# Delta-rule planes stored in pairs, tokens ordered by blocks of four steps, and the whole instruction order written down as a table

## The chip, the cores and the metric

The kernel runs on one core of a Trainium2 chip. Its time is the device time of one execution in microseconds; for the kernel before it is the median of three runs. Lower is better. Profiles are of single executions with the hardware profiler on.

## The reference

The input `x` is 8 sequences of 512 steps with 128 features. Four layers follow one another, each added to its input:

1. a gated linear recurrence over the steps (per channel, `z = a*z + b*u`, with coefficients from the normalised input, and with two weight matrices divided by their largest singular value where that exceeds 1);
2. one linear map, chosen from eight by an argmax over constants;
3. attention by the delta rule with 16 heads of size 8;
4. a mixture of experts: 8 experts 128 to 512 to 128 with a gelu, the best two per token, weighted by their probabilities.

The third layer matters most here. Per head and sequence it keeps an 8 x 8 state:

```
retrieval = einsum('bhij,bhj->bhi', S, k_t)
S = S + einsum('bhi,bhj->bhij', beta_t * (v_t - retrieval), k_t)
o_t = einsum('bhij,bhj->bhi', S, q_t)
```

All data are float32.

## The kernel before

**Tiling.** The 512 steps are cut into 32 tiles of 16 steps (`QT`); a tile has 8 sequences x 16 steps = 128 tokens (`QN`). Eight groups of four tiles (`SIZES`) pass through the layers in turn. The first layer (`scanned`, L814, `ssm_out`, L894), the second (`linear`, L900) and the preparation of the third (`delta_in`, L919) work on a group of 512 tokens at once. Their arrays have features on the partitions and tokens along the free axis, or the reverse after PE transposes. Before all that, two serial chains of 25 matrix squarings (`spectral`, L1445) find the two largest singular values; the second layer's input (`gain`) needs them.

**The recurrence.** `delta_rule` (L1013) works through the tiles in blocks of four steps (`BL`), so 4 blocks a tile and 128 in all. The 128 partitions are 16 heads x 8 rows `i` of the state; the columns of the state are 8 "planes" `j`. `delta_in` writes the normalised queries and keys to DRAM (`scratch`), and two transfers per tile read them back into `kq`, spread so that each partition of a head has all 8 features: 16 planes of 128 tokens. A block is six DVE instructions, each needing the one before it:

- `so = kq * state`: the state at the block's start times keys and queries, 16 planes x 32 tokens = 512 elements;
- `w = sum over planes of so`: the eight key planes and one plane of values (`vals`), nine addends for 32 tokens;
- `prod = tmat * w` and `u4 = sum(prod)`: a prepared 4 x 4 triangular matrix per head resolves the four steps of the block;
- `st = k * u4` and a sum that adds the four steps to the state.

`so` is one array of 26 planes. A plane is 128 neighbouring words, so the nine addends of one token lie 512 bytes apart. Even and odd tiles use different planes for queries and for `vals`, and the same ones for keys. `vals` comes into its plane by a transfer from SP's queue for each tile. After a tile's four blocks, ACT copies `u_16` (the four `u4`) from PSUM to `upd`, POOL multiplies `upd` with the prepared products of queries and keys (`qkp`), from tile 8 on (`PRESUM`) POOL also adds the two halves of the eight query planes of `so`, from tile 28 on also adds `qkp` to them, and PE sums the remaining planes with the output weights `wo` in PSUM. DVE adds the residual (`x3 = po + base`), for each tile, as a step of its own (L1086, the last lines of `delta_rule`).

**Routing and experts.** `route` (L1089) chooses the experts of a group. `experts` (L1190) runs for one group, then three times for two groups, then for the last group (`GROUPS`). It gives every token two places in a table sorted by expert, POOL scatters the rows there with indirect transfers (`places`, L1260), 128-row blocks are loaded (`xb`), their expert's first weights are loaded by a register (`w1b`, five buffers), PE makes the hidden layer (`ph`), ACT the gelu (`hid`), PE the second layer (L1322), ACT copies it (`yb`) and SP stores it (`results`). POOL gathers each token's two rows with indirect transfers (`back`), and POOL or, for the last groups, DVE adds them with their weights into `fin` or `acc`, which goes to `out` by one transfer per tile. There are 99 blocks: 15, 23, 23, 23 and 15.

**What sets the order.** [...] The kernel records all operations first (`Recorder`, L291, `Plan.add`, L112) with what they read and write. `Plan.best` (L189) then places them by `place` (L204): a list scheduler that picks per engine by a rank, with costs from `_cost` (L340) and with due times from a table of one number per stage (`DUE`); `backward` (L144) makes ranks from a first placing. `BURST` and `WINDOW` (L359) can hold indirect transfers apart; here they are 1 and 0, no limit. The four shared PSUM banks (`Bank`) are assigned there too. `emit` (L280) issues everything in that order. Nearly every instruction therefore carries line 316, that of the recorder, and is told apart by its tiles.

**Loads and stores.** A tile of `u` is read by one transfer of 64 KB (`rows_of`, L512, in `load_x`, L516); the token on partition p is sequence p // 16, step p % 16. Each group is read twice, once early for its layer-norm statistics (into a `w1b` buffer) and once for the work. All these are on SP's queue.

Of the kernel before, what the change touches and what calls it, by code (L numbers as in the profile page):

```python
# [9 lines left out]
F32 = mybir.dt.float32  # L10
# [3 lines left out]
ALU = mybir.AluOpType  # L14
AX = mybir.AxisListType

P = 128
# [52 lines left out]
class Plan:  # L70
# [117 lines left out]

    def best(self):  # L189

        stages = sorted({op.key[0] for op in self.ops})
# [148 lines left out]
def _cost(engine, name, n, kw):  # L340
# [7 lines left out]
    if engine == "scalar":  # L348
        columns = sum(isinstance(kw.get(k), bass.AP) for k in ("bias", "scale"))
        return 0.18 + 0.00085 * n + (0.0, 0.0001 * n, 0.13)[columns]  # L350
# [8 lines left out]
BURST, WINDOW = 1, 0.0  # L359
# [5 lines left out]
DUE = (  # L365
    -236, -276.1, -245.3, -238.7, -88.4, -98.3, -52.3, -79.1, -157.5, -15.6, -71, 7.4, -42.8, -28.1, 23.8, 17.7,
    3.3, 15.3, -94.2, -33.2, 126.6, -87.6, -36.7, 39.7, -104.5, -21.9, 9.6, 53.8, 21.8, 117.2, 17.2, 34, 105.7,
    174.3, -88.9, 90.1, 19.1, 146.3, 93.6, 29.9, 38.9, 28.9, 34.5, 209.9, 195.2, 91.1, 102.7, 46.1, 1.8, 95.7,
    -4.3, 89.8, 13.7, 74.3, 96.5, 3.1, 90.5, 77.5, 38.7, 101.6, 143.2, 40.1, -66.1, 12.2, -5.1, 212.4, 20.7, 101.5,
    73.5, 98.5, 116.8, 100.9, 78.2, 3, 102.1, 38.3, 290.5, 128.1, 214.1, 180.9, 131.2, 128, 118.3, 113.8, 15.2,  # L370
    14.5, 225.5, 100.6, 218.2, 210.7, 114.8, 91.1, 105.7, 127.4, 209.4, 212.9, 96.9, 226.6, 177.7, 246.3, 250.5,
    289.6, 287.3, 210.3, 152.1, 215.7, 247.3, 234.5, 176.6, 304.3, 235, 219.2, 187.8, 232.7, 315.6, 194, 205.6,
    295.7, 240.7, 326.7, 206.2, 233.2, 183.6, 211, 284.8, 261.9, 245.8, 311.8, 194.9, 361.5, 272, 302.9, 248,
    136.1, 193.7, 231.9, 225.4, 248.8, 243.7, 247.5, 303.1, 282.2, 193.1, 316, 265, 251.8, 321, 335.7, 373.6,
    307.1, 296.4, 323.7, 318.1, 304.2, 306.2, 317.4, 323.4, 286.7, 304.5, 314.1, 305.1, 311.8, 307, 281.3, 273.9,
    304.9, 267.2, 326.6, 310.3, 341.2, 222.4, 327.2, 320, 342, 274.2, 348.8, 375.1, 433.6, 289.9, 271.2, 406.7,
    316.1, 313, 282.7, 390.3, 246.2, 305.4, 298.8, 320.5, 298.3, 282.6, 219, 458.7, 284.2, 368.8, 326, 305.3,
# [13 lines left out]
def seq_kernel(  # L391
# [120 lines left out]
    def rows_of(dram_, tile):  # L512

        return dram_[:, tile * QT : (tile + 1) * QT, :]
# [1087 lines left out]
```

## Time and profile before

| | us |
|---|---|
| median of 3 runs (lowest, highest) | 699.95 (699.14, 700.88) |
| the profiled execution, its own time | 700.99 |
| its span, first to last instruction | 699.3 |
| busy: PE / DVE / ACT / POOL | 511.3 / 500.4 / 455.1 / 546.4 |
| first block of the recurrence starts | 95.5 |
| last block of the recurrence ends | 591.8 |
| last matmul ends | 681.7 |
| DMA engines' share in use on queue q1 | 51.0% |

"Busy" is the sum over an engine's instructions. A group of instructions reads: line, engine, operation, tile written <- tiles read, shape out <- shape in, count, then busy us and mean ns of one, then the idle time of the engine just before them and what ended it. "issue" is time in which the profile shows no wait. The rows of the page that the prediction shows are not shown again here.

The chain that ended last begins at 647 and is PE's work on the last experts, then POOL's gathers, then DVE's last adds:

```profile
679.89 0.48 ACT yb L316
...
692.33 0.30 issue
692.64 2.87 DMA back<-results,small_dest
...
695.60 0.35 DVE acc L316
```

### The profile page before, as it was taken

What the parts mean: (1) busy time and instruction counts of PE and PEld (TensorE: products, weight loads), DVE (VectorE), ACT (ScalarE), POOL (GpSimd) and SP (SyncE); (2) the same over time, 40 slices, a digit from 0 to 9 for tenths busy, and PEclk for the clock granted to TensorE, in tenths of its full rate; (3) what the DMA queues carried; (4) which work ended last, traced back from release to release, by engine and by line L of the source; (5) the groups of instructions that cost most, each with busy time, mean ns of one, the idle gap of its engine ahead of it and who ended that gap; (6) DMA issues with size and microseconds to landing.
All of it is one profiled execution on the core that took longest, in us unless ns stands there. A gap on an engine that the chain in (4) does not pass through costs nothing. (4 is left out here: it accounts for less than half of the span.)

```text
span 699.3 us, 10984 instructions
## 1 busy us (share of the span) xinstructions
PE 511.3 (73%) x2948; PEld 402.0 (57%) x2948; DVE 500.4 (72%) x1276; ACT 455.1 (65%) x1052; POOL 546.4 (78%) x681
## 2 busy tenths in 40 slices
PE   6883656755783767898569979947799968996990
PEld 5662225433551435677427746836568858986980
DVE  4771199999985999998969999975999987400013
ACT  4987765668763578798495789834675734863660
POOL 7588755896579879898869999977589788777644
PEclk9885686997776689998867997977999989999995
DMA  3492243532264357563557665544787876776762
GB/s 105 132 303 77 62 112 96 129 77 64 65 164 133 87 139 172 154 174 83 139 163 187 176 162 150 148 117 122 209 207 206 244 211 171 207 238 195 211 194 70
DMA packets 97714, 105.92 MB, mean 151 GB/s; under 512 B 9099, under 2 KB 72534, under 8 KB 97654
## 3 DMA queue, kind: packets, MB, share of 16 engines
q1 hardware_dynamic: 92992, 96.66, 51.0%
q0 software_dynamic: 4160, 8.53, 4.3%
q8 instruction: 25, 0.41, 0.3%
q14 instruction: 35, 0.29, 0.1%
q10 hardware_dynamic: 502, 0.03, 0.0%
HBM read 81.26 MB, written 23.94 MB: 150 GB/s over the span
## 5 line engine op out<-in xcount | busy, mean ns | idle before, releaser
L316 ACT ACTIVATE hid<-ph,w1b 128x128 f32<-128x128 f32 x396 | 113.5, 375 | 51.7 <-issue 17.3
L316 PE MATMUL ph<-xbT,w1b 128*128 128x128 f32 x792 | 113.6, 286 | 7.8 <-ACT hid L316 3.6
L316 PEld LDWEIGHTS ph<-xbT,w1b 128*128 128x128 f32 x792 | 103.3, 199 | 21.0 <-ACT hid L316 8.9
L316 DVE TENSOR_TENSOR so<-kq,st 128x512 f32<-128x512 f32 x128 | 87.6, 684 | 7.0 <-DVE st L316 1.1
L1322 PE MATMUL po<-w_sb,hid 128*128 x616 | 86.6, 281 | 6.6 <-ACT hid L316 5.0
L316 DVE TENSOR_REDUCE st<-so 128x32 f32<-128x288 f32 x128 | 84.3, 658 | 3.2
L1322 PEld LDWEIGHTS po<-w_sb,hid 128*128 128x128 f32 x616 | 78.2, 195 | 11.8 <-ACT hid L316 7.3
L316 POOL DMA_INDIRECT back<-results,small_dest x64 | 62.3, 973 | 26.5 <-issue 16.0
L316 PE MATMUL po<-wo,so 128*128 128x128 f32 x304 | 56.5, 344 | 34.1 <-POOL so L316 21.6
L316 PEld LDWEIGHTS po<-wo,so 128*128 128x128 f32 x304 | 51.4, 251 | 49.3 <-POOL so L316 24.8
L1260 POOL DMA_INDIRECT places<-xne,small_dest x64 | 63.9, 998 | 19.0 <-issue 13.3
L316 DVE TENSOR_REDUCE st<-st 128x64 f32<-128x320 f32 x128 | 63.8, 498 | 9.4 <-ACT upd L316 5.2
L316 PE MATMUL in<-b,head_ones 128*128 128x512 f32 x80 | 47.8, 684 | 17.1 <-ACT vals L316 3.4
L285 ACT ACT_TABLE_LOAD x42 | 53.9, 1283 | 6.1 <-DMA hid<-in_L_ffn_b_dram 5.4
L316 DVE TENSOR_TENSOR st<-kq,st 128x256 f32<-128x256 f32 x128 | 54.8, 428 | 4.3
L316 PE MATMUL in<-b,wqkvb 128*128 128x512 f32 x64 | 41.2, 739 | 17.9 <-ACT b L316 6.9
L316 POOL TENSOR_TENSOR qkp<-qkp,upd 128x512 f32<-128x512 f32 x32 | 37.8, 1181 | 12.7 <-ACT upd L316 12.6
L316 PEld LDWEIGHTS po<-wo,qkp 128*128 128x128 f32 x224 | 33.5, 222 | 22.7 <-POOL qkp L316 18.0
L316 PE MATMUL po<-wo,qkp 128*128 128x128 f32 x224 | 36.5, 310 | 13.2 <-POOL qkp L316 13.2
L316 PE MATMUL in<-f,wT 128*128 128x512 f32 x64 | 37.7, 676 | 11.4 <-DVE drive L316 6.0
L316 DVE TENSOR_REDUCE st<-prod 128x32 f32<-128x128 f32 x128 | 37.7, 294 | 9.8 <-ACT upd L316 3.8
L316 DVE TENSOR_TENSOR prod<-tmat,st 128x128 f32<-128x128 f32 x128 | 36.6, 286 | 10.7 <-POOL tmat L316 6.5
(285 smaller groups left out, 1207.0 us busy)
## 6 DMA issues: line engine op xcount, KB each, us to landing
kq<-scratch SPq DMA_DIRECT2D x64, 512.0 KB
w1b<-w1b_dram SPq DMA_DIRECT2D x99, 258.0 KB
xb<-places SPq DMA_DIRECT2D x21, 256.0 KB
results<-yb SPq DMA_DIRECT2D x21, 256.0 KB
places<-yb SPq DMA_DIRECT2D x2, 1472.0 KB
x<-in_L_attn_u_dram SPq DMA_DIRECT2D x32, 64.0 KB
w1b_dram<-in_L_ffn_w_dram SPq DMA_DIRECT2D x1, 2048.0 KB
scratch<-qn SPq DMA_DIRECT2D x8, 256.0 KB
```

What stands on the lines that cost most here:

```text
L285: self.hw.scalar.preload_act_table_set(switch)
L316: return method(*(on(x) for x in args), **{k: on(x) for k, x in kw.items()})
L1260: rows_out = hw.gpsimd.indirect_dma_start(out=table[0 : nblk * P, :], out_offset=bass.IndirectOffsetOnAxis(ap=at, axis=0), in_=src, in_off ...
L1322: return hw.tensor.matmul(out_.on(nc.banks), lhsT=src, rhs=w2_f[:, bass.ds(at + c * P, P)], start=(c == 0), stop=(c == NHB - 1),)
```

## The change

- **Planes in pairs.** `so` becomes two sets (even and odd tiles) of 9 pairs of planes. Two planes of a pair are interleaved word by word: 8 query planes, 8 key planes, and a pair of `vals` and zeros. `so = kq * state` writes every second word; the sum reads five pairs, ten addends, over two axes. PE's weight loads of query planes read every second word.
- **`vals`** comes into its plane by an ACT copy, where a transfer did it.
- **Tokens by blocks.** The token on partition p of a tile is now block p // 32, sequence (p % 32) // 4, step p % 4; a block's 32 tokens are neighbours in `kq`, `so` and `tmat`. `u` is reordered accordingly: for the first group by 16 small loads, alternately from SP and ACT; for the others by one transfer from DRAM to DRAM (`u_rows`) that both later loads read. `out` goes the other way round: one store of a group to `out_rows` and one transfer from there, and for the last group 16 small stores.
- **Buffers.** `xb` 3 to 2, `w1b` 5 to 4, and a temporary of `delta_in` shares another's buffer.
- **The order.** `ORDER` lists the numbers of all recorded operations; `ordered` follows it and gives out the PSUM banks, the one that has been free longest. `DUE` is empty, and the list scheduler doesn't run. `BURST`, `WINDOW` and one cost of `_cost`, which only it reads, change too.

```diff
+    def ordered(self):
+        order, loaded, freed = [], None, list(range(-len(self.banks), 0))
+        for at, number in enumerate(ORDER):
+            op = self.ops[number]
+            for b in op.begins:
+                b.index = min(b.choice, key=freed.__getitem__)
+                freed[b.index] = len(ORDER)
+            for b in op.ends:
+                b.users -= 1
+                if b.users == 0:
+                    freed[b.index] = at
+            switch = op.table if op.table and op.table != loaded else None
+            loaded = switch or loaded
+            order.append((op, switch))
+        return order
...
     def best(self):
+        if len(ORDER) == len(self.ops):
+            return self.ordered()
...
-BURST, WINDOW = 1, 0.0
+BURST, WINDOW = 4, 6.0
...
+    def in_blocks(dram_, g):
+        steps = dram_[:, FROM[g] * QT : FROM[g + 1] * QT, :]
+        return steps.rearrange("b (k t) d -> k b (t d)", t=BL)
+    def blocks_in(rows):
+        return rows.rearrange("q (k b t) d -> (q k) b (t d)", b=B, t=BL)
...
     def load_x(g):
         x = ptile([P, SIZES[g], D], "x", 2)
+        if g:
+            nc.sync.dma_start(x, u_rows[g].rearrange("q p d -> p q d"))
+            return x
         for i in range(SIZES[g]):
-            nc.sync.dma_start(x[:, i], rows_of(u, FROM[g] + i))
+            for k in range(QB):
+                by = nc.sync if k % 2 == 0 else nc.scalar
+                by.dma_start(x[k * B * BL : (k + 1) * B * BL, i], block_rows(u, FROM[g] + i, k))
...
-    so = ctile([P, 26 * QN], "so")
+    so = ctile([P, 2, 2 * DH + 2, QN], "so")
+    nc.gpsimd.memset(so[:, :, 2 * DH :], 0.0)
...
-            nc.sync.dma_start(so[:, v0 * QN : (v0 + 1) * QN], vals[:, cols_q])
-            for x, src in ((xk, scratch[1, q]), (xq, scratch[0, q])):
+            now = so[:, (FROM[g] + q) % 2].rearrange("p x c -> p (x c)")
+            def pairs(x):
+                return now[:, 2 * x * QN : 2 * (x + 1) * QN].rearrange("p (c e) -> p c e", e=2)
+            nc.scalar.copy(pairs(DH)[:, :, 0], vals[:, cols_q])
+            for x, src in ((1, scratch[1, q]), (0, scratch[0, q])):
...
-            so_r = so[:, w0 * QN : (w0 + 9) * QN].rearrange("p (r b t) -> p b t r", b=B, t=QT)
+            so_v = now[:, 0 : 2 * DH * QN].rearrange("p (x c e) -> p x e c", c=QN, e=2)
+            so_r = now[:, DH * QN :].rearrange("p (x c e) -> p c x e", c=QN, e=2)
...
-                nc.vector.tensor_mul(so_v[:, :, :, ts], kq_v[:, :, :, ts], state)
-                nc.vector.tensor_reduce(w, so_r[:, :, ts, :], AX.X, ALU.add)
+                nc.vector.tensor_mul(so_v[:, :, :, ts], kq_v[:, :, ts], state)
+                nc.vector.tensor_reduce(w.rearrange("p b t -> p (b t)"), so_r[:, ts], AX.XY, ALU.add)
...
-            outs = [so[:, (q0 + d) * QN : (q0 + d + 1) * QN] for d in range(DH)]
+            outs = [pairs(d // 2)[:, :, d % 2] for d in range(DH)]
...
+    def rows_out(g, acc):
+        nc.sync.dma_start(out_rows[g].rearrange("q p d -> p q d"), acc)
+        nc.sync.dma_start(in_blocks(out, g), blocks_in(out_rows[g]), group="rows")
...
-                xb = ptile([P, 4, D], "xb", 3)[:, 0:m]
+                xb = ptile([P, 4, D], "xb", 2)[:, 0:m]
...
-            w1b = ptile([P, FW], "w1b", 5)
+            w1b = ptile([P, FW], "w1b", 4)
```

## The prediction

> **What bounds the kernel now.** I read the 40 slices and the costliest groups of the page first, then the groups by form, then the windows by stage, and last the timelines around the long waits.
>
> ```profile
> DVE  4771199999985999998969999975999987400013
> POOL 7588755896579879898869999977589788777644
> ...
> L316 DVE TENSOR_TENSOR so<-kq,st 128x512 f32<-128x512 f32 x128 | 87.6, 684 | 7.0 <-DVE st L316 1.1
> L316 DVE TENSOR_REDUCE st<-so 128x32 f32<-128x288 f32 x128 | 84.3, 658 | 3.2
> L316 DVE TENSOR_REDUCE st<-st 128x64 f32<-128x320 f32 x128 | 63.8, 498 | 9.4 <-ACT upd L316 5.2
> ```
>
> DVE fills the slices from about 90 to 590 us. There it runs a serial chain of 128 blocks (32 tiles of four); one block is six instructions, 684 + 658 + 286 + 294 + 428 + 498 = 2848 ns, and 128 of them 364.5 us. The first starts at 95.5, the last ends at 591.8. So I cut the span into start 95.5, recurrence 496.3, tail 107.5 (699.3 in all); the profiled run's own time, 700.99, has 1.7 more around the span and lies 1.0 above the median of 699.95.
>
> ```profile
> 108.10:589.30 481.20, 358.32 (x2027) 277.26 (x2025) 422.42 (x1011) 321.21 (x704) 399.27 (x495) 0.85 0.56 149
> ```
>
> Columns are window, PE, PEld, DVE, ACT, POOL. From the first to the last product of `qkp`, DVE is busy 422 of 481 us, POOL 399, and POOL's waits add 15.8 us of "issue" after indirect transfers: 415. POOL is second, at 86%. DVE's waits over 0.25 us in the recurrence sum to 29.9 us; four of them, 6.1, 5.2, 3.8 and 8.1, make 23.2. The longest:
>
> ```profile
> 473.70 0.29 DVE L316 TENSOR_TENSOR prod<-tmat,st 128x128 f32<-128x128 f32 x1
> 482.10 0.29 DVE L316 TENSOR_TENSOR x<-po,base 128x128 f32<-128x128 f32 x1 [8.11 <-PE po L316]
> ```
> ```profile
> 473.28 0.97 POOL L1260 DMA_INDIRECT places<-xne,small_dest  x1 [0.30 <-issue]
> 474.56 1.01 POOL L316 DMA_INDIRECT back<-results,small_dest  x1 [0.30 <-issue]
> 475.59 1.27 POOL L316 TENSOR_TENSOR so<-so 128x512 f32<-128x512 f32 x1
> 477.03 1.00 POOL L1260 DMA_INDIRECT places<-xne,small_dest  x1 [0.17 <-issue]
> 478.05 1.20 POOL L316 TENSOR_TENSOR qkp<-qkp,upd 128x512 f32<-128x512 f32 x1
> ```
>
> An add on DVE stands in line for a PE sum, whose `so` and `qkp` planes POOL makes late, behind a train of indirect transfers of 1.27 us each. The other three long waits have such trains beside them too.
>
> [...] From 128 to 320 elements DVE reductions go 294 to 498 ns, 1.06 ns an element on 158 fixed; `st<-so`, whose nine addends lie 512 bytes apart, should take 464 and takes 658. The steps of `tmat` show both cases:
>
> ```profile
> L316 DVE TENSOR_TENSOR b<-b,b 128x128 f32<-128x128 f32 x4 | 1.9, 527 | 0.0
> L316 DVE TENSOR_TENSOR b<-b,beta 128x384 f32<-128x384 f32 x1 | 1.1, 1105 | 10.8 <-ACT b L316 10.8
> L316 DVE TENSOR_TENSOR b<-b,beta 128x256 f32<-128x256 f32 x1 | 0.4, 404 | 0.0
> ```
>
> [...] the product `so<-kq,st` (one PSUM input) stays within 656 to 690 ns over 128 runs, so a busier POOL won't stretch the chain. [...]
>
> **The change, part by part.**
>
> *Reduction by pairs.* `st<-so` now reads five pairs, 320 elements (a zero plane is added)[...]. Value: the row of `st<-st`, also 320, 498 ns. 128 x (658 - 498) = 20.5 us, all in the chain. Bounds: the old excess of 194 ns over 288 elements is 0.67 ns each; if 320 still pay it, 158 + 340 + 215 = 713, +7.0 us in all; a cheaper case than 498 is excluded by the 1.06 ns slope.
>
> *The product writes every second word.* Same 512 elements. [...] Bounds: the excess of 0.67 ns on each would be 343 ns a block, 128 x 0.343 = +44 us; below nothing is excluded, since 684 is already the plain slope (rows of 512 from PE sums also take 680). The other four instructions keep size and count.
>
> *`vals` by an ACT copy.* 32 SP issues of 0.53 us go; 32 copies at the row of `upd` (128x128, 264 ns) come, 8.4 us on ACT, busy 321 of 481. In the built order a tile's copy stands two tiles ahead of its first reduction, before the `upd` copy of two tiles earlier: a cover of about 11 us. It waits for the reduction that last read that plane; queued behind it are the `upd` copy and an activation run. Without cover, 0.3 to 0.5 us a tile, up to +16. I take 0. PE loads `so` planes at a stride of two words: 0, bounded by 128 x 0.67 ns on 160 loads per pass, some 27 us of an engine with 123 us free.
>
> *Tokens by blocks, `u` and `out` in two steps.* 60 loads of 64 KB become 16 small ones and 7 reorderings in DRAM with 14 loads; 28 stores become 7 of 256 KB plus 7 reorderings. That adds some 7.3 MB (7 x 256 KB written and read once more, for `u` and `out`) to 105.9, at a DMA share of 56%: covered, since loads run a group ahead; uncovered each costs some 3 us of landing. But eight of the first loads stand ahead on ACT's queue: its ten issues took from 0.81 to 5.38, 0.46 each, so +3.7; two small steps move behind (-0.7), and ACT idled 1.1 before its first squaring. 1.9 us late, and the squarings are serial: +1.9 (0 to 3).
>
> *Buffers.* `w1b` 5 to 4, `xb` 3 to 2. Four blocks are 4 x 8 matmuls x 0.22 = 7 us of PE, a late `w1b` took 3.9 to land: 0; without that cover 1 to 2 us per late block.
>
> *The table.* It moves work on all queues. The PE order is nearly the same at the end: after the last `so` sum 152 first-layer, 152 second-layer matmuls and 38 transposes, before 144, 152 and 34: +2.7 us at 0.22 a matmul (two of the half passes, of which the chain of waits has 16 in 1.79 us). On POOL the last scatter stands 5.1 us of work later (48.0 after the last `qkp` product where it was 42.9, summed from rows), PE waited 3.6 + 2.1 us there already: +4. The `fin` adds no longer stand behind the last `acc` sum, which held the last gathers to 683.7: -0.7; the last stores on two queues +0.2. Tail +3.5. In the recurrence dependent DVE steps stand further apart, and adds of late sums sit up to twelve blocks after their tile. But indirect transfers are no sparser: at most 11 in any 15 us of POOL work, 10 before, and POOL's work runs up to 20 us behind DVE's (8 before). I let a third of the 23.2 us go: -7.7; bounds -20 and +10.
>
> Sum: 700.99 + 1.9 - 20.5 - 7.7 + 3.5 = 678.2 for a profiled run, 677 as a median.
>
> **Rivals.**
> - *POOL takes over.* DVE's own work falls to some 447 us; POOL's 415 of 481 becomes 415 of 453, 92%, with its trains. What is late next is `qkp` and `so`, then the `upd` copy. Waits grow by 3 in place of falling by 7.7: about 688. For it: the lag of 20 us. Against: adds placed late.
> - *The table cures the waits.* 20 us of them go: 665. For it: all four have one cause; against: the trains remain.
> - *Strided write pays.* At the bound, 677 + 44 = 721: slower. It decides from an excess of 0.19 us a product, (700 - 677)/128, a product of 0.87 us. [...]
> - *Pairs don't help* (the 1105 ns row is the hint): reduction 713 ns, 677 + 20.5 + 7.0 = 704.
>
> **How the numbers follow.** Forecast 0.44, POOL 0.25, cured 0.20, strided write 0.07, pairs 0.04. Below 0.3% (2.1 us) a measurement of this kernel can't tell a change from none. Slower: 0.11; of the POOL case 0.03 reaches 698 to 702; faster 0.86. The range 660 to 694 takes in the first three cases, less their outer ends (0.08), and leaves out 0.11.
>
> **What would show it.** `st<-so` at about 500 ns, 128x320 (wrong at 600 or more); `so<-kq` within 680 to 700; recurrence of 460 to 476 us from the first to the last block; first block at 97; tail of 110 to 112; DVE's long waits near 22 us, named for PE, ACT `upd` or POOL. If POOL takes over, they name POOL `qkp` and `so` and exceed 30. Wrong altogether if the product exceeds 0.87 us, or if waits of the reduction for ACT `so` appear in every tile.

## The result, and the profile after

| | before | after |
|---|---|---|
| median of 15 runs each (lowest, highest) | 701.0 (699.14, 703.48) | 694.65 (690.79, 699.55) |
| the profiled execution, its own time | 700.99 | 694.65 |
| its span | 699.3 | 693.0 |
| start, to the first block | 95.5 | 101.0 |
| recurrence, first to last block | 496.3 | 467.7 |
| tail, from the last block on | 107.5 | 124.3 |

The ratio is 0.991, with a 95% interval of 0.989 to 0.993: faster by 0.9%, where 677 and thus 3.3% had been forecast. The time lies 0.65 us beyond the slow end of the range. The recurrence became shorter by 28.6 us, start and tail longer by 5.5 and 16.8. The recorder's line is 335 in the kernel after, and 340 or 345 in some kernels below.

First the page of the kernel after, the rows that answer to those of before: the slices of DVE and POOL, and the three largest groups of the chain.

```profile
DVE  4565169999997899995899999878999970300111
POOL 5566776699899979998869999987898886786634
...
L335 DVE TENSOR_TENSOR so<-kq,st 128x512 f32<-128x512 f32 x128 | 87.9, 687 | 13.1 <-POOL small_mine L335 7.8
...
L335 DVE TENSOR_REDUCE st<-so 128x32 f32<-128x320 f32 x128 | 63.1, 493 | 4.8
L335 DVE TENSOR_REDUCE st<-st 128x64 f32<-128x320 f32 x128 | 63.6, 497 | 4.0
```

The sum over pairs takes 493 ns where it took 658, and the product, which now writes every second word, 687 where it took 684. The new thing in these rows is the idle time: 7.8 us ahead of one product, named for POOL.

The windows of the recurrence, before and after (columns: window, its length, then busy time of PE, PEld, DVE, ACT, POOL, the granted clock, DMA share, GB/s):

```profile
95.50:591.80 496.30, 367.05 (x2062) 283.58 (x2061) 435.48 (x1039) 330.36 (x723) 406.00 (x503) 0.85 0.55 146
```
```profile
101.00:568.70 467.70, 354.83 (x1988) 270.29 (x1986) 416.77 (x1039) 338.53 (x743) 403.58 (x504) 0.88 0.56 147
```

DVE has 1039 instructions in both. It is busy 18.7 us less and idle 9.9 us less (60.8 before, 50.9 after): together the 28.6. PE has 74 instructions fewer here. They come back in the tail, where the groups of PE by form after the last block show them, before and after:

```profile
L316 PE MATMUL ph<-xbT,w1b 128*128 128x128 f32 x293 | 41.0, 284 | 4.3 <-ACT xbT L316 2.1 <-DMA w1b<-w1b_dram 1.5 <-ACT hid L316 0.6
L1322 PE MATMUL po<-w_sb,hid 128*128 x184 | 24.6, 277 | 0.4 <-ACT hid L316 0.4
```
```profile
L335 PE MATMUL ph<-xbT,w1b 128*128 128x128 f32 x328 | 52.5, 291 | 8.9 <-DMA w1b<-w1b_dram 7.0 <-ACT xbT L335 0.9 <-ACT yb L335 0.7
L1595 PE MATMUL po<-w_sb,hid 128*128 x242 | 37.9, 281 | 0.1
```

A record is a half pass of a matmul: the 99 blocks have 396 first-layer matmuls, and the whole trace 792 records of them. With the second layer's sums under the name `in` (120 and 88), which are not shown, the experts' half passes are 597 before and 658 after: 61 of the 73 that PE has more there. The windows from the last block to the last matmul, before and after, give PE's time:

```profile
591.80:681.70 89.90, 80.37 (x658) 77.10 (x656) 12.12 (x47) 56.40 (x179) 62.04 (x66) 0.96 0.71 207
```
```profile
568.70:673.70 105.00, 92.42 (x731) 87.70 (x731) 12.67 (x56) 62.08 (x196) 69.06 (x71) 0.95 0.73 209
```

Of the 15.1 us more, PE is busy 12.0 and idle 3.1 (12.6 in place of 9.5). Its 73 instructions more, at 80.37 / 658 = 0.122 us each, are 8.9 of the 12.0.

### The profile page after: what moved, and what is told of

It reads as the page before. It is cut to its first block, busy times and chain, and to the rows that moved or that the text cites. A ratio compares the mean times of both kernels' runs of the same rounds, so it can differ in the third digit from the quotient of the medians.

```text
span 693.0 us, 10892 instructions
## 1 busy us (share of the span) xinstructions
PE 514.9 (74%) x2948; PEld 399.2 (58%) x2948; DVE 483.1 (70%) x1276; ACT 465.4 (67%) x1087; POOL 546.3 (79%) x682
## 5 line engine op out<-in xcount | busy, mean ns | idle before, releaser
L335 PE MATMUL ph<-xbT,w1b 128*128 128x128 f32 x792 | 127.9, 292 | 13.3 <-DMA w1b<-w1b_dram 8.0
L335 PEld LDWEIGHTS ph<-xbT,w1b 128*128 128x128 f32 x792 | 112.1, 205 | 25.0 <-issue 11.2
L1595 PE MATMUL po<-w_sb,hid 128*128 x704 | 114.4, 288 | 5.2 <-DVE small_place L335 1.4
L1595 PEld LDWEIGHTS po<-w_sb,hid 128*128 128x128 f32 x704 | 99.1, 201 | 15.7 <-issue 7.5
L335 DVE TENSOR_TENSOR so<-kq,st 128x512 f32<-128x512 f32 x128 | 87.9, 687 | 13.1 <-POOL small_mine L335 7.8
L335 POOL DMA_INDIRECT back<-results,small_dest x64 | 61.9, 968 | 32.9 <-DMA results<-yb 16.2
L335 PEld LDWEIGHTS po<-wo,so 128*128 128x128 f32 x264 | 45.5, 239 | 36.4 <-issue 17.7
L335 DVE TENSOR_REDUCE st<-so 128x32 f32<-128x320 f32 x128 | 63.1, 493 | 4.8
L335 PE MATMUL po<-wo,so 128*128 128x128 f32 x264 | 51.8, 333 | 19.1 <-DVE x L335 7.9
L335 PE MATMUL in<-f,wT 128*128 128x512 f32 x64 | 41.8, 750 | 10.8 <-DVE x L335 4.4
L335 DVE SCALAR_TENSOR_TENSOR fin<-back,small_weight,fin 128x128 f32<-128x128 f32 x16 | 5.1, 349 | 57.4 <-DMA back<-results,small_dest 50.1
L335 POOL TENSOR_TENSOR so<-so 128x512 f32<-128x512 f32 x24 | 30.7, 1280 | 12.1 <-DVE so L335 10.7
```

The lines of the kernel that those rows point to most:

```text
L335: return method(*(on(x) for x in args), **{k: on(x) for k, x in kw.items()})
L1595: return hw.tensor.matmul(out_.on(nc.banks), lhsT=src, rhs=w2_f[:, bass.ds(at + c * P, P)], start=(c == 0), stop=(c == NHB - 1),)
```

## What was tried

Three questions: what the 7.8 us wait is and what it costs; what made the start 5.5 us later; why PE has more left at the end. The table has the stages of a profiled execution of most kernels; those with other buffers, other places for loads or half the columns are told in the last part. On two of the chips (one of them marked *) every kernel, the one before included, took some 30 us longer (the one before 733.89 and 730.69, on the others 699.96 to 701.88), with stops common to several engines in the tail, of up to 17 us: there only the ratio and the stages up to the last block are compared with other chips.

| kernel | first block | recurrence | last matmul after it | median | ratio to before, 95% |
|---|---|---|---|---|---|
| before | 95.5 | 496.3 | 89.9 | 701.0 | |
| after | 101.0 | 467.7 | 105.0 | 694.65 | 0.991 (0.989 to 0.993) |
| after, again | 101.4 | 467.3 | 103.6 | 693.71 | 0.990 (0.985 to 0.994) |
| POOL held to the table* | 99.7 | 460.4 | 126.2 | 709.36 | 0.967 (0.962 to 0.972) |
| first loads all on SP* | 105.2 | 466.9 | 129.0 | 722.9 | 0.985 (0.980 to 0.991) |
| last copy first* | 99.8 | 472.9 | 127.1 | 720.84 | 0.981 (0.976 to 0.986) |
| first group in two transfers | 98.3 | 468.4 | 105.2 | 691.78 | 0.986 (0.983 to 0.990) |
| POOL held, and two transfers | 98.5 | 461.5 | 100.2 | 680.92 | 0.971 (0.967 to 0.975) |
| the same, again | 100.2 | 459.5 | 102.0 | 681.81 | 0.973 (0.969 to 0.976) |
| nine planes apart | 100.4 | 478.3 | 102.5 | 704.53 | 1.007 (1.005 to 1.009) |
| ten planes apart (one run) | 101.3 | 483.7 | 102.9 | 708.93 | |
| new layout, old scheduler | 105.6 | 523.9 | 101.0 | 749.99 | 1.073 (1.070 to 1.076) |

### The wait for POOL

The timelines around it, of POOL, ACT, PE and DVE, of the kernel after (start, duration, instruction, idle time before it):

```profile
311.94 1.10 POOL L1533 DMA_INDIRECT places<-xne,small_dest  x1 [0.17 <-DVE st L335]
...
322.18 0.96 POOL L1533 DMA_INDIRECT places<-xne,small_dest  x1 [0.31 <-issue]
323.16 2.48 POOL L335 TENSOR_TENSOR both<-f,f 128x512 f32<-128x512 f32 x2
```
```profile
325.68 1.06 ACT L335 ACTIVATE both<-both 128x1024 f32<-128x1024 f32 x1 [8.58 <-POOL both L335]
326.64 1.25 ACT L335 ACTIVATE f<-in,dbias 128x512 f32<-128x512 f32 x2
```
```profile
327.94 0.80 PE L335 MATMUL in<-wo,so 128*128 128x128 f32 x2 [9.08 <-ACT f L335]
...
328.96 1.49 PE L335 MATMUL in<-wo,so 128*128 128x128 f32 x6
```
```profile
322.24 0.50 DVE L335 TENSOR_REDUCE st<-st 128x64 f32<-128x320 f32 x1
330.54 0.69 DVE L335 TENSOR_TENSOR so<-kq,st 128x512 f32<-128x512 f32 x1 [7.80 <-POOL small_mine L335]
```

Nine scatters follow one another, 1.27 us each with the 0.30 of "issue". POOL's `both`, of a later group's first layer, stands behind them; ACT waits 8.58 us for it and then, with `f`, empties a PSUM bank (`in`); PE waits 9.08 us for that and then sums a tile's `so` planes, until 330.45. Counted through, DVE's next product is the first of tile 15 (of 0 to 31), which writes the set of planes that this sum, of tile 13, reads. It starts at 330.54, after 7.80 us. The profile names POOL's `small_mine`, which ended at the same moment; in the kernel with the planes apart, below, it puts the like wait (6.67 us) down to PE `in`. That the product waits for this sum is read from the four timelines; the profile does not say it. The table has at most four scatters in a row. In the trace of the program as built there are trains of nine and seven: the scatters of a group are declared independent of one another, and then nothing holds a scatter that stands directly behind another one to its place, so that it is built ahead of POOL's other work. On POOL, then, the order is not the table's. The experiment makes it so: a scatter waits, in issue order only, for what stands ahead of its run of scatters.

```diff
                 made = op.emit()
                 if op.engine == "gpsimd":
-                    self.tc.keep_in_program_order(made)
+                    for name in behind if op.group is None else behind[:1]:
+                        self.tc.add_manual_dep(made.ins, name, issue, reason="the table's order")
+                    behind = [made.ins.name] if op.group is None else behind + [made.ins.name]
```

> POOL's queue as built does not follow the table: a row scatter that the table puts directly behind another row scatter is free to move ahead, so nine of them stand in a row at 312 us and eight at 555, where the table has at most four. This kernel holds POOL to the table and changes nothing else. My theory: DVE's wait of 7.80 us at 330 goes or falls below 3, PE's wait of 5.66 us for the sum planes `so` of the last tile but one goes; recurrence 461 to 463 in place of 467.7, tail 118 to 120 in place of 124.3; 682 to 685 in place of 694.65. Rival 1, the tail is plain PE work (61 more expert matmuls than before behind the last block) and POOL only fills gaps: recurrence as above, tail 123 to 125, about 689. Rival 2, POOL is short of time and the waits only move: 694, long DVE waits still above 20 us.

The wait is gone and the recurrence is 460.4. PE's wait of 5.66 us for `so` at the end is now two, of 1.26 and 1.08. What it gains in the whole is measured below, on a chip without the common stops.

### The start

ACT's timeline from the first instruction to the first squaring, before and after:

```profile
0.81 0.55 ACTq L316 DMA_DIRECT2D hid<-in_L_attn_bp_dram  x1
...
8.02 0.40 ACT L316 ACTIVATE xne<-acc,sp 128x128 f32<-128x128 f32 x1 [1.12 <-DVE sp L316]
```
```profile
0.81 6.34 ACTq L335 DMA_DIRECT2D x<-in_L_attn_u_dram  x8
7.19 0.64 ACTq L335 DMA_DIRECT2D hid<-in_L_attn_bp_dram  x1
...
12.57 0.40 ACT L335 ACTIVATE xne<-acc,sp 128x128 f32<-128x128 f32 x1
```

The eight issues of `u` took 6.34 us, 0.79 each, and all that ACT did followed 6.4 us later. If only ACT's queue were the trouble, they could go to SP:

```diff
-                by = nc.sync if k % 2 == 0 else nc.scalar
+                by = nc.sync
```

> All sixteen first loads of `u` are issued by SP; ACT's queue begins with its ten small loads as before the change. My theory: ACT's first squaring step starts at 8.0 to 8.5 in place of 12.57, the first block of the recurrence at 96 to 97 in place of 101.0, and all of it is passed to the end: 690. Rival 1, SP's own queue takes the place: the first rows and weights land 4 us later, the first block stays at 100 to 101, 694. Rival 2, the start is 5 us earlier and the tail that much longer, since PE's backlog of experts is what ends: 693 to 695.

The first block came at 105.2, some 4 us later than with both queues: the rival holds. SP's timeline of this kernel says why:

```profile
1.28 0.86 SPq L335 DMA_DIRECT2D x<-in_L_attn_u_dram  x1
2.18 0.39 SPq L335 DMA_DIRECT2D acc<-in_L_attn_W_in_dram  x1
2.61 4.22 SPq L335 DMA_DIRECT2D x<-in_L_attn_u_dram  x6
6.88 0.44 SPq L335 DMA_DIRECT2D hid<-in_L_attn_Wp_dram  x1
```

The weights `Wp` go out at 6.88, behind seven small loads. Sixteen small issues cost 0.7 to 0.9 us each on either queue, so the number has to fall: for the first group too, one reordering in DRAM and one load.

```diff
-        if g:
-            nc.sync.dma_start(x, u_rows[g].rearrange("q p d -> p q d"))
-            return x
...
+        if g == 0:
+            nc.sync.dma_start(blocks_in(u_rows[g]), in_blocks(u, g))
+        nc.sync.dma_start(x, u_rows[g].rearrange("q p d -> p q d"))
...
+ORDER = (1, 0, 2, 4, 3) + tuple(n - 14 for n in ORDER if n > 18)
```

> The first group of `u` comes by one reordering transfer in DRAM and one load, as the other groups do, in place of sixteen small loads; ACT's queue begins with its ten small loads. My theory after the run with all sixteen on SP: what costs is the issue of sixteen small transfers, 0.79 us each on either queue (6.34 us for eight on ACT), and who issues them only decides who waits. Here two issues take their place: first squaring step of ACT at 8.0 to 9.0 in place of 12.57, first block at 96 to 98 in place of 101.0, 3 to 5 us off the total. Rival: the two hops land so late (7 to 9 us) that DVE, whose statistics of `u` stand ahead of the squarings' scale, starts the squarings at 11 to 12 all the same: first block at 100 to 101, total unchanged.

The first block came at 98.3, the time fell by 1.9, where 3 to 5 had been expected, against the kernel after on the same chip (its own repetition follows).

> The changed kernel once more, unaltered, as the measure for the kernels beside it. The chip of the four runs before was slower in the tail of every kernel, the kernel before among them (733.9 in place of 701.0), with stops of PE, ACT and SP together of up to 17 us that the first profiles don't have. If that is the chip, this kernel gives 0.991 of the kernel before on a chip like the first, and about 0.98 on one like the second; its recurrence is 467 to 469 us on either.

It gave 693.71, the first result again. So 3 us of start gave 2 in the end, within what two medians differ by.

### Both edits together

> POOL held to the table, and the first group by two transfers. Without stops in the tail: first block at 96 to 98, recurrence 460 to 461 (it was 460.4 with POOL held to the table, 467.7 without), tail 118 to 121 where PE's wait of 5.66 us for `so` is gone; 677 to 681 on a chip like the first, 0.97 of the kernel before. If the tail is PE's backlog alone, every us that the recurrence ends earlier is a us more of tail, and the total stays within 3 us of the changed kernel's.

680.92, as expected, and 681.81 in a repetition below. PE's waits for the last two `so` sums did not go altogether: they are 3.15 and 1.98 us here, the second in the tail. POOL's timeline at the same place, and DVE's group of products over the page:

```profile
311.60 1.10 POOL L1537 DMA_INDIRECT places<-xne,small_dest  x1 [0.16 <-DVE st L340]
...
314.27 0.96 POOL L1537 DMA_INDIRECT places<-xne,small_dest  x1 [0.30 <-issue]
315.25 2.49 POOL L340 TENSOR_TENSOR both<-f,f 128x512 f32<-128x512 f32 x2
317.70 1.18 POOL L340 TENSOR_TENSOR qkp<-qkp,upd 128x512 f32<-128x512 f32 x1
```
```profile
L340 DVE TENSOR_TENSOR so<-kq,st 128x512 f32<-128x512 f32 x128 | 87.9, 687 | 4.8 <-DVE st L340 0.8
```

Three scatters, then `both` and `qkp`; PE's sum of `so` starts at 320.04 and DVE's product after it waits only 0.19 us. Over the page, idle time ahead of the product falls from 13.1 to 4.8. DVE's waits over 0.25 us in the recurrence sum to 11.8 us (29.9 before, 23.2 after). This version beats both kernels: of the 13 us that it gains over the kernel after, the one with two transfers alone has 2, so holding POOL to the table is worth about 11. The kernel before has trains too, of seven, six, six and five scatters; no run holds its POOL to its own order, so what the same edit would be worth there is not known.

### What the pairs are worth

The kernel after with nine planes that lie side by side, as before, and all else kept:

```diff
-            def pairs(x):
-                return now[:, 2 * x * QN : 2 * (x + 1) * QN].rearrange("p (c e) -> p c e", e=2)
+            def plane(x):
+                return now[:, x * QN : (x + 1) * QN]
...
-            so_r = now[:, DH * QN :].rearrange("p (x c e) -> p c x e", c=QN, e=2)
+            so_r = now[:, DH * QN : (DH + 9) * QN].rearrange("p (x c) -> p c x", c=QN)
```

> The changed kernel with the pairs undone and all else kept: every plane of `so` is 128 neighbouring words again, the product writes them without stride and the reduction reads nine addends 512 bytes apart. Theory of the pairs: `st<-so` takes 650 to 665 ns for 288 elements in place of 493 for 320, the product stays at 684 to 690, the recurrence is 20 to 21 us longer, 488; total 710 to 715, or less if the tail then has less left over. Rival, the chain has slack in it: recurrence below 478.

The reduction takes 662 ns (row below), as before the change, and the chain 21 us more (groups of the recurrence: 364.4, 343.2). The recurrence takes 478.3, only 10.6 more, just beyond the rival's bound of 478 and far from the 488 of the theory; the median is 704.53, where 710 to 715 had been expected. Its window shows where the rest is:

```profile
L335 DVE TENSOR_REDUCE st<-so 128x32 f32<-128x288 f32 x128 | 84.7, 662 | 4.8
```
```profile
100.40:578.80 478.40, 357.01 (x1988) 270.68 (x1987) 432.94 (x1039) 339.68 (x743) 404.15 (x506) 0.88 0.54 144
```

Against the kernel after, DVE is busy 16.2 us more, not 21, since its small instructions beside the chain took less (92.8 in place of 97.8, summed from the groups); and it is idle 45.5 in place of 50.9. Its waits over 0.25 us sum to 17.5 in place of 23.2. So part of what the shorter chain saves is waited for.

Ten planes apart, the element count of the pairs without their layout:

```diff
-            so_r = now[:, DH * QN : (DH + 9) * QN].rearrange("p (x c) -> p c x", c=QN)
+            so_r = now[:, DH * QN : (DH + 10) * QN].rearrange("p (x c) -> p c x", c=QN)
```

> As the kernel with the planes apart, but the reduction reads ten of them (the plane of zeros too), the 320 elements that the pairs read. If every element of an unpaired reduction pays the excess of 0.67 ns, `st<-so` takes 710 to 720 ns; if the excess is a fixed one of about 195 ns for the instruction, 690 to 697.

```profile
L335 DVE TENSOR_REDUCE st<-so 128x32 f32<-128x320 f32 x128 | 91.8, 717 | 4.8
```

717 ns for 320 elements apart, 493 for 320 in pairs: the layout alone is worth 224 ns, and the penalty goes by the element, as the prediction's bound of 713 had it.

### What the table is worth

The new layout, without the table, and with the due times and limits of before:

```diff
-BURST, WINDOW = 4, 6.0
+BURST, WINDOW = 1, 0.0
...
+ORDER = ()
```

> The changed kernel without its table: the list scheduler runs with the due times, costs and limits of the kernel before, on the new layout, with four buffers. If the tail's extra length is the table's choice: first block at 98 to 102, recurrence 474 to 480 (496.3 less the reduction's 20.5, waits of 25 to 33 us), tail 108 to 113, 683 to 692. If a faster chain leaves PE that much more of the experts' work in any order: the same recurrence, tail 118 to 126, 692 to 703.

749.99, which neither theory had: recurrence 523.9, first block 105.6, DVE's long waits 63.7 us, the largest 11.65 (ACT `upd`) and 9.89 (PE `po`). Due times that were found for one layout do not fit another, so this run does not price the table by itself. It shows that the layout with the old due times is 7% slower than before. Its tail is long as well: 118.5 us, with 634 of the experts' half passes after the last block.

### The end of the table, and the tail

The first suspect was a late copy of the last `upd` on ACT (576.93), with the last add behind it:

```diff
+ORDER = moved(ORDER, 4566, 4564)
```

> The last tile's copy of `u_16` to `upd` on ACT, which started at 576.93 behind an experts' copy although its data were there at 567.7, is put ahead of that copy; nothing else moves. Theory of ACT's queue: the last residual add comes 8 us earlier, tail 115 to 117, 686. Theory of PE's queue (mine): the last sum on PE stands behind some 60 expert matmuls that PE worked without a gap from 571.1 to 580.4 and can't start before them; the copy was late for nobody: tail 123.5 to 124.5, 694 to 695.

The copy starts 4 us earlier, 472.1 us after the first block where it was 476.0 in the kernel after. But DVE's last sum of the recurrence now waits for it:

```profile
572.13 0.50 DVE L335 TENSOR_REDUCE st<-st 128x64 f32<-128x320 f32 x1 [4.47 <-ACT upd L335]
```

So the recurrence is 472.9, and the last block is no landmark here. Counted from the first block, PE's last `so` sum starts at 479.0 in place of 479.5 and the last add at 480.2 in place of 480.7: neither follows the copy. That is the theory of PE's queue; the late copy is not what sets the end.

Next the buffers of `w1b`, since PE waits 7 to 8 us for loads of it in the tail. The straightforward edit:

```diff
-            w1b = ptile([P, FW], "w1b", 4)
+            w1b = ptile([P, FW], "w1b", 5)
...
-        of_block = gtile([1, MAXB, NE], "of_block")[:, 0:nblk]
+        of_block = ptile([1, MAXB, NE], "x3T")[:, 0:nblk]
```

> Five buffers for the experts' first weights, as before the change, and a small array moved into another's buffer to make room. My theory: of PE's 8.0 us of waits for `w1b` in the tail about 6 go, the tail is 118 to 120 in place of 124.3, the recurrence is unchanged, 688 to 690. Rival: the transfers are late because the queues are full (DMA share 0.7 to 0.8 in the tail), not because a buffer is missing: the waits stay at 6 to 8 us and the time at 693 to 695.

> The same with five buffers for the experts' first weights. Theory of the missing buffer: PE's waits for `w1b` in the tail, 8.0 us in the changed kernel's first profile, fall below 2, and the total is 4 to 6 below the kernel with POOL held to the table and the two transfers. Rival, full DMA queues: the waits stay, the total is within 2 us of it.

731.15 (ratio 0.998, 0.995 to 1.000, on a chip with stops) and 693.53 (0.989, 0.985 to 0.994), the second 12.6 slower than the same without the fifth buffer. Neither answers the question. The table was made for four buffers; with five, 17 loads stand in it ahead of an activation that still has its bias in the buffer, so that, as we read the table, in these two kernels a few activations take the bias of a later block, and wait for its load (16.8 us on ACT between 440 and 560 in the second). A version in which an operation is held until what it depends on has been placed:

```diff
+        table, held = {}, []
+        for number in ORDER:
+            held.append(self.ops[number])
+            for op in list(held):
+                if all(o in table for o in op.after):
+                    table[op] = held.remove(op)
```

> POOL held to the table, the first group by two transfers, and five buffers for the experts' first weights, with the table mended: the table was made for four buffers, and with five some loads stood ahead of an activation that still reads the buffer, so that the two earlier kernels with five buffers waited for a later block's load there and took its bias for a few columns. Here each load is put behind those readers. Theory of the missing buffer: PE's waits for `w1b` in the tail fall from 7.6 to below 3 us and the time to 675 to 678 on a chip like the first (0.964 to 0.968 of the kernel before). Rival, full DMA queues: they stay at 6 to 8 us and the time at 679 to 683 (0.969 to 0.974).

721.74 (1.030, 1.026 to 1.033), with one wait of PE of 29.12 us for `w1b` at 668. The fault was again in the edit: the small array `of_block`, from which the blocks' experts are read, shared a buffer with `x3T` and so stood behind work that it has nothing to do with. With the buffers placed where nothing waits (`of_block` in that of `chosen`, a second small array in another's):

> POOL held to the table, the first group by two transfers, and five buffers for the experts' first weights; room for them comes from two small arrays that share the buffers of arrays dead by then, and the seventeen loads that the table, made for four buffers, puts ahead of an activation still reading their buffer are put behind it. Theory of the missing buffer: PE's waits for `w1b` in the tail fall from 7.6 us to below 3, the tail by 4 to 6 us, the ratio to the kernel before from 0.971 to about 0.964. Rival, full DMA queues: waits stay at 6 to 8 us, ratio 0.969 to 0.973.

> The kernel with POOL held to the table and the first group by two transfers once more, as the control of the kernel beside it: ratio 0.967 to 0.975 to the kernel before, recurrence 461, tail 119 to 121, PE's waits for `w1b` in the tail 7 to 8 us.

682.5 (0.972, 0.967 to 0.976) with five buffers and 681.81 with four; PE waits 6.9 and 8.2 us for `w1b`. The missing buffer costs nothing that the total shows, as the prediction had it. The mended table lengthens this kernel's recurrence (464.2 against 459.5 in the control), while its last matmul comes 99.2 us after the last block in place of 102.0, so that a gain of one to three us in the tail alone is not excluded. In the trace with five buffers SP's queue is what stands still:

```profile
593.82 0.38 SPq L345 DMA_DIRECT2D out_rows<-fin  x1
...
596.33 0.36 SPq L345 DMA_DIRECT2D fin<-kept  x1
597.25 0.35 SPq L1584 DMA_DIRECT2D w1b<-w1b_dram  x1
```

SP waits 4.9 us ahead of the first of these for POOL's `fin`, and 1.5 ahead of the next (`fin<-kept`); loads of `w1b` stand behind. So nine such transfers were moved behind the next loads, with four buffers and with five:

```diff
+for number, behind in ((2227, 4156), (3288, 4169), (2228, 4182), (3301, 4243), (3302, 4262),
+                       (3303, 4277), (3316, 4706), (4309, 4719), (3317, 4732)):
+    ORDER = moved(ORDER, number, behind)
```

> POOL held to the table, the first group by two transfers, four buffers; on SP's queue the stores to `out_rows`, their second transfers and the loads of `fin` of three groups in the tail stand behind the next two to four loads of the experts' weights, which they stood ahead of. Theory of SP's line: PE's waits for `w1b` in the tail fall from 8 us to below 4, the tail from 120 or 122 to 116 or 117, the ratio to 0.966. If line and buffer are both needed: waits 6 to 8, ratio 0.970 to 0.974. Full DMA queues: the same 6 to 8.

> The same move on SP's queue with five buffers. If line and buffer are both needed, the waits fall below 3 us here and not with four buffers, and the ratio is 0.963 to 0.966. Full DMA queues: waits 6 us or more here too, ratio 0.970 to 0.974.

> The kernel with the stores to `out_rows` behind the loads of weights, four buffers, once more. On a chip where the kernel before takes 700 us: theory of SP's line, PE's waits for `w1b` in the tail below 4 us, tail 115 to 117, 675 to 678, ratio 0.964 to 0.967; otherwise waits 6 to 8, tail 119 to 122, 680 to 682, ratio 0.970 to 0.974. On a chip where the kernel before takes 730 us: 704 to 709, and the question stays open.

The first two fell on a chip with common stops (706.92, 0.966, 0.962 to 0.970; 710.5, 0.971, 0.966 to 0.975). The waits for `w1b` were 5.6 and 3.6 us there. The ratio of the first could hide half a per cent of gain, so it was run again on another chip: 682.8 (0.973, 0.970 to 0.976), with 8.4 us of waits. No gain over 680.92 and 681.81: SP's line is not the cause either. The traces tell one thing more. One of the six loads that PE waits for in the tail of the kernel after, its issue by SP and the matmul that waited for it:

```profile
608.78 0.37 SPq L1575 DMA_DIRECT2D w1b<-w1b_dram  x1
```
```profile
613.48 0.71 PE L335 MATMUL ph<-xbT,w1b 128*128 128x128 f32 x4 [2.01 <-DMA w1b<-w1b_dram]
```

From issue to that matmul it is 4.70 us here, 3.4 to 5.0 in all six, and 4.0 to 5.1 for the three such loads of the kernel before (as the profile pairs loads and matmuls). A load that PE waits for takes no longer than before; it is issued later than PE needs it. That speaks against full DMA queues. What delays the issue stays open.

Last, whether the tail goes by PE's work. In the last two groups each expert matmul gets 64 of its 128 columns: the hidden layer leaves out half of the tokens, the second layer half of the output features.

```diff
+                n = P // 2 if last > 20 else P
...
-                    ph[:, cs], lhsT=w1b[:, cs], rhs=xbTs[j0][:, i * P : (i + 1) * P], start=True, stop=True
+                    ph[:, c * P : c * P + n], lhsT=w1b[:, cs], rhs=xbTs[j0][:, i * P : i * P + n], start=True, stop=True
```

> POOL held to the table, the first group by two transfers, and in the last two expert groups (38 blocks) every matmul moves 64 of its 128 columns, so that half of the tokens' expert results in these groups are left out; all transfers, activations and POOL's work stay. If PE's backlog sets the tail: some 600 half passes at 0.11 less each, tail 119.7 less 20 to 40, until ACT, POOL or the transfers hold it; 640 to 660. If the transfers of `w1b` or POOL's indirect transfers set it: tail 112 or more, above 670.

727.35 (of two runs, 722.31 and 732.39; 1.039, 1.030 to 1.047), which no theory had. Windows of the tail, full and half columns:

```profile
600.00:640.00 40.00, 36.10 (x293) 35.00 (x293) 0.35 (x1) 23.64 (x78) 27.14 (x27) 0.96 0.85 251
```
```profile
570.00:580.00 10.00, 9.71 (x47) 9.72 (x47) 0.00 (x0) 5.17 (x17) 7.49 (x10) 0.50 0.65 186
600.00:640.00 40.00, 40.00 (x190) 40.00 (x190) 3.17 (x21) 16.68 (x50) 23.74 (x23) 0.50 0.56 161
```

The granted clock was 0.50 from about 570 on (0.86 in the ten us before); PE did 190 instructions, nearly all of them half passes, in 40 us where it did 293, and waited for no `w1b` at all. As a test of columns it is spoiled, but it tells two things. With a slower PE the tail is longer: the last matmul comes 152.7 us after the last block in place of 100.2. And fewer columns did not make up for the clock: a half pass of 64 columns took 40.00 / 190 = 0.21 us, one of 128 columns 36.10 / 293 = 0.123. The weight loads' mean rose from 196 to 325 ns, so that they, not the columns, seem to set the pace; that is an inference.

## Why the prediction was right in the recurrence and wrong at both ends

| term | forecast | measured |
|---|---|---|
| start | +1.9 | +5.5 |
| recurrence: pairs -20.5, waits -7.7 | -28.2 | -28.6 |
| tail | +3.5 | +16.8 |
| profiled execution | 678.2 | 694.65 |

The differences, 3.6 - 0.4 + 13.3, make the 16.5 us. The forecast of the tail has a slip of its own: its four terms, 2.7 + 4 - 0.7 + 0.2, make 6.2, and the 3.5 leaves out the first. With it the profiled execution would have been put at 680.9, still 13.8 us short.

**The reduction by pairs: right.** That five pairs would take what `st<-st` takes was an estimate from that row; 493 ns where 498 was taken, so 128 x (658 - 493) = 21.1 us out of the chain. That the recurrence gained just what the sum said is partly luck. The chain became 21.5 us shorter, but DVE's busy time only 18.7: its other instructions, as many as before, took 97.8 us where they had 88.1 (groups of the two windows; many overlap with the chain). The long waits gave 6.7 where 7.7 had been put, and 3.2 came from short waits that nobody had forecast. Undoing the pairs alone costs 10.6 us, not 21.

**The strided write, ACT's copy of `vals`, PE's strided loads: right at nothing.** That the write would cost nothing was the author's estimate: the product took 687 ns where it took 684, and the bound of +44 us is excluded. No reduction waits for ACT `so`. PE's strided loads have no run of their own.

**Readings in it that do not hold.** The four `b<-b,b` of 527 ns on average (128 elements, single words four words apart) took 899, 422, 396 and 390: the mean rests on one slow instruction that ran beside POOL's work. Three of them still took about what 256 elements in pairs took (404), so the direction holds. The row of 1105 ns (384 elements in runs of three), taken for a hint that pairs don't help, ran beside POOL's work from beginning to end, so that it can't tell what runs of three cost. DVE's "own work" of 447 us is not its busy time, which fell from 435.48 to 416.77. And (700 - 677)/128 is 0.18, not 0.19.

**The third of the long waits: the size right, the reason only in part.** 23.2 us are left in place of 29.9, beside 22 forecast. Of the prediction's sentence "the trains remain" the runs show more than it said: they remained because the built program doesn't follow the table on POOL. The prediction read the built order, and so counted eleven indirect transfers in 15 us correctly (the trace has eleven from 552 on); it did not compare it with the table, which has no more than four scatters in a row. With POOL held to the table there are still ten in 15 us, so that count does not tell the two apart. The single wait of 7.80 us stands behind such a train, and holding POOL to the table takes it away. Of the rivals, "POOL takes over" names the right engine (the profile puts the three longest waits, 14.2 of the 23.2 us, down to POOL, though not to `qkp` or `so`) but not the size, "the table cures the waits" describes the kernel that POOL's order would have given: its 20 us are close to the 18.1 that are gone (29.9 to 11.8) in the version held to the table.

**The start: a term mis-sized.** "0.46 each, so +3.7" was the price of ACT's other small loads; the loads of `u` took 0.79 each, 6.34 in all. The deductions (1.1 of idle time, 0.7 of steps moved behind) fit: 6.34 less these is 4.54, and the first squaring came 4.55 late, and the first block came 5.5 late, all of that and a little more. With two transfers in place of sixteen the first block is back at 98.3.

**The tail: the step that failed.** The prediction counted what PE has to do "after the last `so` sum", found 152 and 152 matmuls where there were 144 and 152, and priced the difference at +2.7. That count was right: from that sum to the last matmul it is 93.3 us after and 89.6 before. What it took for granted, and put at nothing, is that this sum stands as close to the last block as before. Before it began 0.3 us after the last block:

```profile
592.12 1.06 PE L316 MATMUL po<-wo,so 128*128 128x128 f32 x8
```

After, PE's timeline shows it 11.7 us later than the last block (568.7), behind a wait for POOL and behind expert matmuls:

```profile
571.09 0.80 PE L335 MATMUL in<-wo,so 128*128 128x128 f32 x2 [5.66 <-POOL so L335]
571.68 1.06 PE L335 MATMUL ph<-xbT,w1b 128*128 128x128 f32 x4
...
578.64 1.95 PE L1595 MATMUL po<-w_sb,hid 128*128 x16
580.42 1.10 PE L335 MATMUL po<-wo,so 128*128 128x128 f32 x8
```

So of the 16.8 us, 11.4 are this delay, 3.7 the work after it, and 1.7 the gathers and adds that close the kernel (17.6 to 19.3 after the last matmul), where -0.5 had been forecast; why these grew is not shown. The delay has two parts: 2.4 us of the wait that lie after the last block, behind the train of scatters that POOL has at 556 to 565, and 9.3 us of work that the table has put between the last sums: 58 instructions, 50 of them experts' half passes, at a granted clock of 0.71. The window from the last block to that sum:

```profile
568.70:580.40 11.70, 9.31 (x58) 9.31 (x59) 0.29 (x1) 4.18 (x14) 7.48 (x7) 0.71 0.31 85
```

With POOL held to the table the sum comes 7.6 us after the last block, and the last matmul 100.2 after it in place of 105.0. What remains is in the order: with nine planes apart the recurrence is 10.6 us longer, and PE still has the same 658 experts' half passes after the last block, since they stand in its queue behind sums that the chain sets free. So a recurrence that ends 28 us sooner does not bring PE's experts along, and a longer one does not let them go ahead. Whether another order would is not shown: the one kernel without the table, with old due times and a slower recurrence, has 634 left. The +4 that the prediction put in for POOL stood for a late scatter at the end; what the runs show is a late sum in front.

Not settled: why PE waits 7 to 8 us for loads of `w1b` in the tail, where it waited 1.5 before. An earlier place in SP's queue does not help, and a fifth buffer shows no gain. The DMA engines are fuller there (a share of 0.82 between 600 and 640, 0.71 in the like stretch before, 620 to 660), but the loads that PE waits for take no longer from issue to use.

## What to carry to other kernels

Compare the order that was built with the order that was written, engine by engine: a declared independence can undo the written order, and here restoring it was worth 11 us, more than the change itself gained. A wait's name is where to begin: follow the timelines of the other engines to what really ends it. When a chain on one engine becomes shorter, count what another engine has left from the end of that chain on, not from a landmark whose place the change moves too. Here few, large first transfers mattered more than which queue issued them (first block at 98.3 with two transfers, at 101.0 with sixteen from two queues, at 105.2 with sixteen from one), and a first price for a transfer's issue has to come from one of its own shape (0.79 us where 0.46 had been taken).

## What the runs showed of the hardware

- The DVE reduction over words 512 bytes apart took 662 ns for 288 elements and 717 for 320 (one run), and 493 for 320 when two neighbours are read together. The product took 687 ns with a write at a stride of two words, and 684 without it.
- A small DVE instruction took 3.12 us beside POOL's work. DVE's timeline of the version with both edits:

```profile
315.80 3.12 DVE L340 TENSOR_SCALAR small_where<-small_expert 1x23 int32<-1x23 f32 x1
```

  The same instruction takes 0.16 at 439.52. The long one ends at 318.92, when POOL's `both` and `qkp` (shown above, to 318.88) are done. What held it is not shown. The product `so<-kq,st`, with one input from PSUM, took 656 to 690 ns in its 128 runs before and 657 to 712 after.
- An issue of the small loads of `u` took 0.79 us on ACT's queue, more than the 0.46 of others. With all sixteen on SP's queue, at 0.7 to 0.9 us each, the first block came at 105.2 in place of 101.0.
- With half the columns in the experts' matmuls of the tail the granted clock was 0.50 in the windows from 570 to 640 (0.778 as the mean of the whole execution), with PE busy 141.2 of the 142.0 us from 570 to 712, and the kernel became 7% slower than with all columns. Why the clock fell is not shown.
